# Five edits at the end of an attention kernel: a move split over two queues, a reordered reciprocal and addition, copies by another engine, a last output in halves

## The chip, the cores and the metric

The kernel runs on one core of one Trainium2 chip. The metric is the device time of one execution in microseconds; before the change it is 1126.27 us, the median of three runs (1125.67 to 1128.89). A core has five engines that run their own instruction lists in order and wait for each other by semaphores: TensorE (PE in the profile, its weight loads PEld), VectorE (DVE), ScalarE (ACT), GpSimd (POOL) and SyncE (SP), which here only issues transfers (DMAs). ACT can issue transfers too. Matrix products are summed up in PSUM, other data lie in SBUF.

## What is computed

64 batches of 128 tokens of 512 features pass through one attention layer with a residual. There are 16 heads of 64, one key and one value for all heads, a learned null key and value in front, a causal mask and a mask of tokens. The output is normalized before it is added to the input:

```python
xn = layernorm(x, g_in)
q = (xn @ Wq).reshape(b, n, H, DH).transpose(0, 2, 1, 3) * scale
k, v = split(xn @ Wkv)                      # null key and value put in front
sim = einsum('bhid,bjd->bhij', q, k) + bias # causal and token masks
attn = softmax(sim, axis=-1)
out = einsum('bhij,bjd->bhid', attn, v).transpose(0, 2, 1, 3).reshape(b, n, INNER)
return x + layernorm(out @ Wo, g_out)
```

All arithmetic is float32.

## The kernel before, in words

The order of all instructions is written out by hand. `step(n)` runs for n from -6 to 62, and each step holds work for several batches at different stages: the projections of later batches, the softmax of batch `eb`, the scores of batch `nb`, the values of batch n, and the output of batches before. In the last steps eb = n + 2 and nb = n + 3. With B = 64, B3 = 58. Behind step 62 a few lines finish batches 62 and 63. The lists of the engines keep the order in which `step` calls its helpers.

For one batch b the stages are these:

- `scores` (L495) multiplies queries and keys on PE into `ps`, one buffer, in two halves of the queries; `scores_add` (L508, DVE) adds them to the tile `s`, which POOL has filled with bias and masks; `scores_max` (L513, DVE) takes the maxima. A later half's scores can only start when the addition has read `ps`.
- `exps` (L522, ACT) takes the exponentials, one instruction for each of 8 rows in each half, and sums them. `rinv` (L539, DVE) is the reciprocal of the sums and `scale` (L543, POOL) multiplies by it.
- `blocks_T` (L575, DVE) transposes blocks of 32x32 from `s` into `sb`, and `blocks_move` (L601) moves them in 14 transfers into `aTb`. There are two tiles `aTb` for the last batches, used in turn. With `take=0` only the even-numbered seven of the transfers are issued, by SP; with `take=1` the odd-numbered seven, by ACT. Before the change only batch 63 is split in this way.
- `values` and `values_end` (L636, PE) multiply `aTb` with the values into two tiles `po`, and two copies with a bias (L680, ACT) bring them to `oT`.
- The output product with `wo`: up to batch 58 two batches at a time, by a scheme with seven products of half size (`out_sums` on POOL, `out_product` L750 on PE, `out_part` L773 on DVE, or L771 on ACT). Then follow `pair_stats`, the power -0.5 on POOL (`pair_pow`), `pair_nmr` (L794, DVE), `pair_norm` (L804, ACT into `yn`) and `pair_residual` (L808 and L809, DVE). From batch 59 on it is `out_mm` (L697, PE: 8 products of 512 columns into `py`), `out_stats` (L813 to L820, DVE), `residual` (L834 on ACT, L835 on POOL), `store` (L838, SP).

The residual's input is loaded a second time into `res`, of which there are two buffers (L126, SP): the load for a batch must wait until the batch two before it in these loads has been added. SP's list in steps 59 and 60 is: moves of 60, res(58), res(59), moves of 61, stores of 57 and 58, res(60), moves of 62, SP's half of the moves of 63. ACT's list from step 58: yn(55), first half of the exponentials of 60, oT(58), yn(56), second half of 60, all of 61 (with one copy between), oT(59), exponentials of 62 with the copy that completes y(58) and yn(57) between, yn(58), oT(60), the residual of 59, exponentials of 63, oT(61), seven moves of 63, the residual of 60, oT(62).

Of the kernel before, what the change touches and what calls it, by code (L numbers as in the profile page):

```python
# [17 lines left out]
def kernel(  # L18
# [654 lines left out]
    def values_end(b, split):  # L673
        g = b // GB
        if split:
            value_mm(b, 1, 1, lo, vs[g], slice(4, 6), start=False)
            value_mm(b, 0, 1, hi, vs[g], slice(2, 4), start=False)
        po = pos.pop(b)
        for u in range(2):
            nc.scalar.activation(  # L680
                oT[b][:, u * NF : (u + 1) * NF, :].rearrange(
                    "p f (s q) -> p s f q", q=Q
                ),
                po[u].rearrange("p h i f q -> p (h i) f q"),
                AF.Identity,
                bias=nv2,
            )

    def out_mm(b, lo=0, hi=NC):
        if lo == 0:  # L690
# [44 lines left out]
    def out_product(p, k, pool, tag, start=True):  # L735
        key = "y" + tag
        if start:
            prod[key] = pool.tile([P, HE], FP, tag=tag, name=f"py{tag}_{p}_{k}")
        a, b = oT[p], oT[p + 1] if p + 1 in oT else None
        h, w = {  # L740
            1: lambda: (a[:, lo_c], e11),
            2: lambda: (a[:, hi_c], e21),
            3: lambda: (a[:, hi_c], e22),
            4: lambda: (b[:, hi_c], wT[:, 3]),
            5: lambda: (yS[p], wT[:, 0]),
            6: lambda: (a[:, lo_c], wT[:, 1]),
            7: lambda: (b[:, lo_c], wT[:, 2]),
        }[k]()
        for c in range(HC):
            nc.tensor.matmul(  # L750
                prod[key],
                h[:, c, :],
                w[:, c, :],
                start=(start and c == 0),
                stop=(c == HC - 1),
                skip_group_check=not start,
            )
# [39 lines left out]
    def pair_norm(b):  # L797
        if b not in nmrs:
            pair_nmr(b)
        nmr, rstd = nmrs.pop(b)  # L800


        yn[b] = ps_y.tile([P, DIM], FP, tag="Y", name=f"yn_{b}")
        nc.scalar.activation(yn[b], ys[b], AF.Identity, bias=nmr, scale=rstd)  # L804
# [6 lines left out]
    def out_stats(b):  # L811
        st = small.tile([P, 6], FP, tag="st", name=f"sto_{b}")
        nc.vector.bn_stats(st, ys[b])  # L813
        mv = small.tile([P, 2], FP, tag="mvo", name=f"mvo_{b}")
        nc.vector.bn_aggr(mv, st)
        rstd = small.tile([P, 1], FP, tag="rstdo", name=f"rstdo_{b}")
        nc.vector.tensor_scalar(rstd, mv[:, 1:2], EPS, None, ALU.add)
        nc.gpsimd.tensor_tensor(rstd, rstd, nhalf, ALU.pow)
        y = hp.tile([P, DIM], FP, tag="y", name=f"y_{b}", bufs=3)
        nc.vector.scalar_tensor_tensor(  # L820
            y, ys.pop(b), mv[:, 0:1], gob, ALU.subtract, ALU.mult
        )
        if b == B - 1:

            nc.vector.scalar_tensor_tensor(y, y, rstd, res.pop(b), ALU.mult, ALU.add)
        else:
            yr[b] = y, rstd
        ys[b] = y

    yr = {}  # L830
# [1 line left out]
    def residual(b):  # L832
        y, rstd = yr.pop(b)
        nc.scalar.activation(y, y, AF.Copy, scale=rstd)  # L834
        nc.gpsimd.tensor_tensor(y, y, res.pop(b), ALU.add)  # L835

    def store(b):
        nc.sync.dma_start(out=out[b], in_=ys.pop(b))  # L838
# [40 lines left out]
    def step(n):  # L879
# [131 lines left out]
        if n == B3:  # L1011
            out_keep("X", "yp1", "p1")
            scores(eb, 0)
            scores_add(eb, 0)
            scores_max(eb, 0)
            out_product(p12, 2, ps_w, "w")
            pair_norm(p4)
            pair_residual(p4)
            store(p4)
            out_part(p12, 0, "w", "yp1")  # L1020
            scores(eb, 1)
            scores_add(eb, 1)
            exps_half(eb, 0)
            scores_max(eb, 1)
        elif first:
            out_keep("X", "yp1", "p1")
            out_product(p12, 2, ps_w, "w")
            out_part(p12, 0, "w", "yp1")
# [7 lines left out]
            q_out(qg, f, lo_t, "w", "p1")  # L1036
        if soft and not second:
            exps(eb, 1, 6)
            rinv(eb, 1)
            scale(eb, 1)  # L1040
        if third and n != B3:
            pair_norm(p4 + 1)
        if second:
# [2 lines left out]
        if n == B3 + 1:  # L1046
            rinv(eb, 0)
            scale(eb, 0)
            blocks_T(n + 1)
            blocks_move(n + 1)  # L1050
        if soft and second:
            exps(eb, 1, 4)
            rinv(eb, 1)
            scale(eb, 1)
        for m in mns:
# [28 lines left out]
            pair_nmr(p4 + 1)  # L1084
        if ok(n):
            values(n, split)
        if third and n != B3:
            pair_residual(p4 + 1)
            store(p4 + 1)
        if soft:  # L1090
            blocks_T(eb)
        if sc and n != B3:
            scores_max(nb, 0)
# [2 lines left out]
            keep("a", "u2")  # L1096
        if ok(n) and not split:
            values_end(n, split)
            if n > B3 + 1:
                out_mm(n - 1, NF)  # L1100
        if n == B3:
# [140 lines left out]
    out_stats(B - 2)  # L1242
    residual(B - 2)
    store(B - 2)
    out_mm(B - 1)
    out_stats(B - 1)
    store(B - 1)
# [1 line left out]
_INS = [  # L1249
    "x",  # L1250
# [34 lines left out]
```

## Time and profile before

| | |
|---|---|
| median of three runs | 1126.27 us |
| profiled execution, own time | 1131.23 us |
| its span, first to last instruction | 1129.4 us |
| mean granted TensorE clock | 0.995 |
| busy: PE, DVE, ACT, POOL | 96%, 72%, 60%, 66% |
| matmuls busy, 1040 to 1060 us | 18.15 of 20.00 us |
| 1060 to 1080 | 17.89 of 20.00 |
| 1080 to 1100 | 18.37 of 20.00, clock 0.91 |
| 1100 to 1130 | 22.44 of 30.00, clock 0.98 |

A row of the timeline gives the start in us from the start of the span, how long the group of instructions took, the engine, the line of the code, the operation, what it writes and reads, the shape and the count; in brackets how long the engine had been idle before it and which instruction released it. SPq and ACTq are the issues of transfers by SP and ACT. A row of the waits gives who waited for whom, the total in us, how often, and the longest. A row of stretches gives the stretch, its length, the busy time of PE, PEld, DVE, ACT and POOL (with counts), the granted clock (1.00 is full), the share of the transfer engines and GB/s.

### The profile page before, as it was taken

What the parts mean: (1) busy time and instruction counts of PE and PEld (TensorE: products, weight loads), DVE (VectorE), ACT (ScalarE), POOL (GpSimd) and SP (SyncE); (2) the same over time, 40 slices, a digit from 0 to 9 for tenths busy, and PEclk for the clock granted to TensorE, in tenths of its full rate; (3) what the DMA queues carried; (4) which work ended last, traced back from release to release, by engine and by line L of the source; (5) the groups of instructions that cost most, each with busy time, mean ns of one, the idle gap of its engine ahead of it and who ended that gap; (6) DMA issues with size and microseconds to landing.
All of it is one profiled execution on the core that took longest, in us unless ns stands there. A gap on an engine that the chain in (4) does not pass through costs nothing.

```text
span 1129.4 us, 27505 instructions
## 1 busy us (share of the span) xinstructions
PE 1089.5 (96%) x9780; PEld 873.0 (77%) x9780; DVE 808.0 (72%) x1741; ACT 678.1 (60%) x2710; POOL 745.3 (66%) x588
## 2 busy tenths in 40 slices
PE   6988999999999999999999999999999999999987
PEld 4565788888888888788888888888888888888643
DVE  6564677777787777678777768877777886666852
ACT  2345656666765666676565667566566756657651
POOL 5454877767675776767577676757768575777832
PEclk9999999999999999999999999999999999999999
DMA  6313244363454436345343533534353353422333
GB/s 186 121 33 96 63 128 115 93 168 98 128 131 127 118 91 169 98 124 133 122 123 91 165 105 120 132 120 118 100 163 104 125 134 99 114 75 76 96 104 101
DMA packets 107864, 130.09 MB, mean 115 GB/s; under 512 B 29264, under 2 KB 72528, under 8 KB 105936
## 3 DMA queue, kind: packets, MB, share of 16 engines
q1 hardware_dynamic: 106480, 126.96, 40.0%
q8 instruction: 78, 1.28, 0.5%
q10 hardware_dynamic: 1248, 1.38, 0.4%
q14 instruction: 58, 0.48, 0.1%
HBM read 54.86 MB, written 31.46 MB: 76 GB/s over the span
## 4 chain that ended last, share of the span: by engine, by line
PE 68%; DMA 8%; POOL 7%; DVE 6%; SPq 5%; issue 3%; ACT 3%; POOLq 0%; ACTq 0%; DVEq 0%
PE pa L422 14%; PE pyX L750 13%; PE pc L422 7%; PE ps L495 7%; PE po L636 6%; PE pyY L750 6%; DMA x<-in_x_dram 6%; PE pk L308 4%; SPq L601 4%; PE pw L422 3%; PE pyw L750 3%; PE py L697 3%; ACT s L522 2%; POOL s L543 1%; POOL xS L404 1%
## 5 line engine op out<-in xcount | busy, mean ns | idle before, releaser
L522 ACT ACTIVATE s<-s,nmax 128x65 f32<-128x65 f32 (+1 forms) x1024 | 372.2, 368 | 0.4
L466 POOL TENSOR_TENSOR s<-biasp,mneg 128x1536 f32<-128x1536 f32 x64 | 221.1, 3455 | 110.0 <-DVE sb L575 99.0
L543 POOL TENSOR_TENSOR s<-s,rinv 128x512 f32<-128x512 f32 (+1 forms) x128 | 189.2, 1479 | 119.5 <-DVE nmro L794 86.8
L680 ACT ACTIVATE oT<-po,nv 128x512 f32<-128x512 f32 x128 | 81.0, 683 | 203.2 <-PE po L636 203.2
L522 ACT ACTIVATION_READ_ACCUMULATOR s<-s,nmax 128x1 f32 x1024 | 195.2, 191 | 0.0
L750 PE MATMUL pyX<-wT,oT 128*128 128x256 f32 x696 | 164.7, 379 | 0.5 <-DVE kyu L762 0.5
L750 PEld LDWEIGHTS pyX<-wT,oT 128*128 128x128 f32 x696 | 131.9, 190 | 19.4 <-DVE kyu L762 0.9
L508 DVE TENSOR_TENSOR s<-ps,s 128x512 f32<-128x512 f32 (+1 forms) x128 | 121.6, 950 | 14.2 <-PE ps L495 13.3
L495 PEld LDWEIGHTS ps<-kT,qT 64*64 64x64 f32 x4096 | 92.2, 134 | 46.8 <-DVE s L508 24.9
L422 PE MATMUL pa<-xS,wq 128*128 128x256 f32 x480 | 123.7, 380 | 2.0 <-POOL wq L390 1.0
L513 DVE TENSOR_REDUCE nmax<-s 128x8 f32<-128x520 f32 (+1 forms) x128 | 120.2, 939 | 5.1 <-POOL s L475 3.7
L495 PE MATMUL ps<-kT,qT 64*64 64x64 f32 (+1 forms) x4096 | 116.6, 251 | 3.3 <-DVE s L508 2.6
L575 DVE STREAM_TRANSPOSE sb<-s 128x1536 f32<-128x1536 f32 x62 | 110.0, 1774 | 11.6 <-POOL s L543 4.6
L636 PE MATMUL po<-aTb,vs 64*64 64x256 f32 (+1 forms) x1240 | 114.2, 380 | 2.2 <-DVE done L668 2.2
L433 ACT COPY ku<-pa 128x256 f32<-128x256 f32 x120 | 44.7, 372 | 94.4 <-PE pa L422 94.4
L422 PEld LDWEIGHTS pa<-xS,wq 128*128 128x128 f32 x480 | 86.7, 190 | 12.2 <-ACT ku L433 1.6
L308 PE MATMUL pk<-wkv,xT 128*128 128x144 f32 x488 | 70.2, 287 | 0.0
L422 PE MATMUL pc<-xS,wS 128*128 128x256 f32 x240 | 63.2, 386 | 6.9 <-POOL xS L404 6.9
L422 PE MATMUL pa<-xS,wS 128*128 128x256 f32 x240 | 68.8, 409 | 0.0
L443 DVE TENSOR_TENSOR qT<-pw,kp 128x256 f32<-128x256 f32 x60 | 25.4, 424 | 59.8 <-ACT kp L433 59.7
L636 PEld LDWEIGHTS po<-aTb,vs 64*64 64x64 f32 (+1 forms) x1240 | 55.9, 134 | 12.2 <-issue 3.8
L246 POOL TENSOR_TENSOR rstd<-rstd,nhalf 128x1 f32<-128x1 f32 x64 | 35.8, 559 | 44.5 <-DVE rstd L245 44.4
(120 smaller groups left out, 2105.9 us busy)
## 6 DMA issues: line engine op xcount, KB each, us to landing
aTb<-sb SPq DMA_DIRECT2D x369, 64.0 KB
x<-in_x_dram SPq DMA_DIRECT2D x64, 256.0 KB
res<-in_x_dram SPq DMA_DIRECT2D x64, 256.0 KB
out_dram<-y SPq DMA_DIRECT2D x64, 256.0 KB
aTb<-sb SPq DMA_DIRECT2D x492, 32.0 KB
xd<-xb SPq DMA_DIRECT2D x14, 1024.0 KB
xT<-xd SPq DMA_DIRECT2D x56, 256.0 KB
wo<-in_L_cond_Wo_dram SPq DMA_DIRECT2D x1, 2048.0 KB
```

The lines of the kernel that those rows point to most:

```text
L308: nc.tensor.matmul(pkv, xT[g][:, t, kc, :], wkv[:, kc, :], start=(kc == 0), stop=(kc == KC - 1),)
L422: nc.tensor.matmul(prod[tag], w[:, kc, f * P : (f + 1) * P], t[:, :, kc, :], start=(start and kc == 0), stop=(kc == HK - 1), skip_group_ch ...
L466: nc.gpsimd.tensor_tensor(S[b][:, :, 1 : ROW - 1], biasp, mneg[g][:, t].unsqueeze(1).broadcast_to([P, R8, NL + N]), ALU.add,)
L495: nc.tensor.matmul(pv[u * DH : (u + 1) * DH, r, f, :], qT[g][rows, f, t, hf, u], kT[b][rows, 0:nk], start=True, stop=True,)
L508: nc.vector.tensor_tensor(sv, pss.pop((b, hf)), sv, ALU.add)
L513: nc.vector.tensor_reduce(nmax[b][:, hf], S[b][:, :, WITH_NULL[hf]], AX.X, ALU.max, negate=True)
L522: nc.scalar.activation(row, row, AF.Exp, bias=nmax[b][:, hf, k : k + 1], accum_out=rsum[b][:, hf, k : k + 1],)
L543: nc.gpsimd.tensor_tensor(sv, sv, rinvs.pop((b, hf)).unsqueeze(2).broadcast_to([P, R8, sv.shape[2]]), ALU.mult,)
L575: nc.vector.transpose(sb.rearrange("p j e q -> p e j q"), S[b][:, :, 1 : ROW - 1].rearrange("p e (j k) -> p e j k", k=Q),)
L636: nc.tensor.matmul(pos[b][u][r * DH : (r + 1) * DH, half], vals[keys, b % GB, 0:DH], aT_of(b)[keys, slots, r * NF : (r + 1) * NF], start=s ...
L680: nc.scalar.activation(oT[b][:, u * NF : (u + 1) * NF, :].rearrange("p f (s q) -> p s f q", q=Q), po[u].rearrange("p h i f q -> p (h i) f q"),
L750: nc.tensor.matmul(prod[key], h[:, c, :], w[:, c, :], start=(start and c == 0), stop=(c == HC - 1), skip_group_check=not start,)
```

## The change

Five edits, all at the end of the program.

1. In step 58 `out_part(57, 0)`, the first half of the features of y(57), comes ahead of the norm, residual and store of batch 55.
2. In step 59 the moves of batch 60 are split: seven are issued by SP at the old place, and seven by ACT behind the exponentials of batch 61. Before, SP issued all 14.
3. In step 60 the reciprocal and the scaling of the second half of batch 62 come behind the addition of the scores of batch 63 and the values of 60. In step 61 those of batch 63, and its transposes, come behind the values and the copies of batch 61.
4. The two copies of `values_end` are made by DVE for batches 61 and 62.
5. The output of batch 63 is computed in two halves of 256 features, each with 8 products into a PSUM tile of its own. Statistics are taken of each half and aggregated, the subtraction, the multiplication and the addition run for each half, and each half has its own store.

```diff
@@ values_end
         for u in range(2):
-            nc.scalar.activation(
-                oT[b][:, u * NF : (u + 1) * NF, :].rearrange(
-                    "p f (s q) -> p s f q", q=Q
-                ),
-                po[u].rearrange("p h i f q -> p (h i) f q"),
-                AF.Identity,
-                bias=nv2,
-            )
+            o = oT[b][:, u * NF : (u + 1) * NF, :].rearrange("p f (s q) -> p s f q", q=Q)
+            v = po[u].rearrange("p h i f q -> p (h i) f q")
+            if b in (B - 3, B - 2):
+                nc.vector.tensor_scalar(o, v, nv2, None, ALU.add)
+            else:
+                nc.scalar.activation(o, v, AF.Identity, bias=nv2)
@@ out_stats
-        if b == B - 1:
-            nc.vector.scalar_tensor_tensor(y, y, rstd, res.pop(b), ALU.mult, ALU.add)
-        else:
-            yr[b] = y, rstd
+        yr[b] = y, rstd
@@
+    def last_output():
+        b = B - 1
+        halves = []
+        st = small.tile([P, 2, 6], FP, tag="st2", name="st2", bufs=1)
+        for e, (pool, tag) in enumerate(((ps_y, "Y"), (ps_w, "w"))):
+            cols = (lo_e, hi_e)[e]
+            py = pool.tile([P, HE], FP, tag=tag, name=f"py_{b}_{e}")
+            for c in range(NC):
+                nc.tensor.matmul(
+                    py,
+                    oT[b][:, c, :],
+                    wo[:, c, cols],
+                    start=(c == 0),
+                    stop=(c == NC - 1),
+                )
+            nc.vector.bn_stats(st[:, e], py)
+            halves.append((py, cols))
+        mv = small.tile([P, 2], FP, tag="mvo", name=f"mvo_{b}")
+        nc.vector.bn_aggr(mv, st)
+        rstd = small.tile([P, 1], FP, tag="rstdo", name=f"rstdo_{b}")
+        nc.vector.tensor_scalar(rstd, mv[:, 1:2], EPS, None, ALU.add)
+        nc.gpsimd.tensor_tensor(rstd, rstd, nhalf, ALU.pow)
+        y = hp.tile([P, DIM], FP, tag="y", name=f"y_{b}", bufs=3)
+        for py, cols in halves:
+            nc.vector.scalar_tensor_tensor(
+                y[:, cols], py, mv[:, 0:1], gob[:, cols], ALU.subtract, ALU.mult
+            )
+        r = res.pop(b)
+        for py, cols in halves:
+            nc.vector.scalar_tensor_tensor(
+                y[:, cols], y[:, cols], rstd, r[:, cols], ALU.mult, ALU.add
+            )
+            nc.sync.dma_start(out=out[b][:, cols], in_=y[:, cols])
@@ step
             out_product(p12, 2, ps_w, "w")
+            out_part(p12, 0, "w", "yp1")
             pair_norm(p4)
             pair_residual(p4)
             store(p4)
-            out_part(p12, 0, "w", "yp1")
             scores(eb, 1)
@@
         if soft and not second:
             exps(eb, 1, 6)
-            rinv(eb, 1)
-            scale(eb, 1)
+            if n <= B3 + 1:
+                rinv(eb, 1)
+                scale(eb, 1)
@@
             blocks_T(n + 1)
-            blocks_move(n + 1)
+            blocks_move(n + 1, take=0)
         if soft and second:
             exps(eb, 1, 4)
+            if n == B3 + 1:
+                blocks_move(n + 1, take=1)
             rinv(eb, 1)
             scale(eb, 1)
@@
             values(n, split)
+        if n == B3 + 2:
+            rinv(eb, 1)
+            scale(eb, 1)
         if third and n != B3:
             pair_residual(p4 + 1)
             store(p4 + 1)
-        if soft:
+        if soft and n != B3 + 3:
             blocks_T(eb)
@@
             values_end(n, split)
+            if n == B3 + 3:
+                rinv(eb, 1)
+                scale(eb, 1)
+                blocks_T(eb)
             if n > B3 + 1:
                 out_mm(n - 1, NF)
@@ end of the program
-    out_mm(B - 1)
-    out_stats(B - 1)
-    store(B - 1)
+    last_output()
```

## The prediction

> **What bounds the kernel now.** I read the end of the program only, since every edit lies behind 1050 us. Times are us from the start of the span (1129.4), and I name work by its batch. First the timeline: TensorE (PE) has work without a break up to 1054 us, and from there these are its larger gaps, with the instruction that ended each:
>
> ```profile
> 1055.39 0.65 PE L636 MATMUL po<-aTb,nv 64*64 64x256 f32 x4 [0.89 <-DVE y L773]
> 1056.67 1.26 ACT L680 ACTIVATE oT<-po,nv 128x512 f32<-128x512 f32 x2 [0.42 <-PE po L636]
> ...
> 1078.58 0.43 PE L636 MATMUL po<-aTb,nv 64*64 64x256 f32 x2 [0.92 <-DMA aTb<-sb]
> ...
> 1081.32 1.98 PE L495 MATMUL ps<-kT,qT 64*64 64x128 f32 x32 [1.66 <-DVE s L508]
> ...
> 1097.06 3.70 PE L697 MATMUL py<-wo,oT 128*128 128x512 f32 x8 [0.31 <-ACT oT L680]
> ...
> 1102.14 0.65 PE L636 MATMUL po<-aTb,nv 64*64 64x256 f32 x4 [0.80 <-DMA aTb<-sb]
> ...
> 1108.04 3.70 PE L697 MATMUL py<-wo,oT 128*128 128x512 f32 x8 [0.61 <-ACT oT L680]
> ```
>
> In order: the values of 58 wait for VectorE (DVE), those of 60 for their moves, the scores of 63 for an addition, the output of 61 for oT, the values of 62 for their moves, the output of 62 for oT. The reader should see how small they are: 5.2 us in all. Behind 1108 nothing waits until the tail.
>
> Next the sync queue (SP), because the chain of waits runs through it from 1093 to 1102 us, issue by issue:
>
> ```profile
> 1067.15 9.89 SPq L601 DMA_DIRECT2D aTb<-sb  x14
> 1077.09 2.74 SPq L126 DMA_DIRECT2D res<-in_x_dram  x2
> 1079.92 9.91 SPq L601 DMA_DIRECT2D aTb<-sb  x14
> 1089.88 1.09 SPq L838 DMA_DIRECT2D out_dram<-y  x2
> 1091.01 0.46 SPq L126 DMA_DIRECT2D res<-in_x_dram  x1
> 1091.58 15.74 SPq L601 DMA_DIRECT2D aTb<-sb  x21
> ```
>
> These are the moves of 60, the loads res(58) and res(59), the moves of 61, two stores, res(60), then the moves of 62 and half of those of 63. From 1079.9 on SP issues without rest, and the last move of 62 lands at 1102.05, which ends the 0.80 wait. So **the start of the moves of 61 sets the end**. What sets that start is in the list of SP's waits:
>
> ```profile
> SPq L126 <- DVE y L809: 1.7, 1, 1.7
> ```
>
> res(59) needs the buffer of res(57), free when DVE has added y(57), 1078.77 to 1079.46. Then come 22 us of SP work. Anything that delays y(57) arrives at the end; SP being done sooner with 60 doesn't help while it waits there.
>
> Last, stretches of 3.41 us laid on the clock's own steps (PE busy, ..., granted clock):
>
> ```profile
> 1057.41:1060.82 3.41, 2.12 (x55) 1.62 (x46) 3.06 (x7) 3.40 (x13) 2.95 (x4) 1.00 0.24 59
> ...
> 1077.89:1081.30 3.41, 1.08 (x12) 0.57 (x12) 2.31 (x6) 3.00 (x14) 1.48 (x3) 1.00 0.51 133
> 1081.30:1084.71 3.41, 3.39 (x41) 2.51 (x42) 3.13 (x5) 0.73 (x2) 1.27 (x1) 0.50 0.36 97
> ```
>
> After a stretch with 1.08 us of matmuls the next one ran at half clock, which costs half of 3.41, 1.7 us; after one with 2.12 it did not.
>
> **The change part by part.**
>
> *1. Half of y(57) ahead of the norm of 55 (step 58).* DVE now has to take L773 before nmro(55). L773 reads pyw, whose matmuls end at 1051.05 + 1.99 = 1053.04. So L773 (0.41) runs 1053.08 to 1053.49, nmro ends at 1053.62, and ScalarE (ACT) starts yn(55) at 1053.65 instead of 1052.77: 0.88 late. The eight exponentials of 60 behind it end at about 57.1, so oT(58) starts there and not at 1056.67, although its values, freed from the 0.89 wait, are ready about 0.5 sooner than before. On DVE the reciprocal of (60, first half) waits for those exponentials, 57.2 instead of 56.38, and pushes the maxima and nmro(56) from 57.64 to 58.46. ACT takes yn(56) at 58.69, not 57.94: **0.75 late**. From there ACT has no gap up to the last exponential of 61 at 1067.78, so 0.75 stays, and with it the transposes of 60 and 61. Ends: -0.4 (if only the 0.42 wait of oT goes) and +0.88. I take +0.75, because each link is an in-order queue with its own row.
>
> *2. Moves of 60 from two queues (step 59).* Seven of 14 leave SP; SP is done at about 1072.5 instead of 1077.0 and then waits at res(59) as before. ACT issues the other seven behind the exponentials of 61 (1067.87 + 0.75 = 68.6) and ahead of oT(59). The nearest row is the move of 63, which already goes this way:
>
> ```profile
> 1100.56 6.03 ACTq L601 DMA_DIRECT2D aTb<-sb  x7
> ```
>
> Seven issues held ACT for 6.03 us, the shortest 0.60, the median 0.74, one of 1.43. ACT was free from 1067.9 to 1071.39 (3.52 of wait for the values of 59), so that much is hidden and no more. With seven at 0.74 (5.2) ACT is free at 73.85. Queued behind: oT(59) (1.26), four exponentials of 62 (1.35), the copy that completes y(58), six more exponentials; then yn(57). So oT(59) 73.9 to 75.15, y(58) at 76.85, the exponentials to 78.9, yn(57) at 78.93 instead of 1077.22: 1.71 late, 0.96 of it from this edit. At 0.60 plus gaps (4.5 us) it would be 0.2, at 6.03 it is 1.85. I take the median, **+0.96**.
>
> The Trainium skill speaks against this edit. "DMA: Bandwidth & Descriptors", section "Issuing engines are not separate DMA queues", says that issuing from several engines saves only the time of issuing. By the rows, two queues took 6.7 us for 63 and one took 9.9 for 60; 3.2 sooner would remove the 0.92 wait of the values of 60, and the edit would come to +0.96 - 0.92, nearly nothing. By the rule only SP's issue time is saved, and SP spends that waiting for y(57): +0.96 stays. I take the rule's sum, since the removed wait lies before the SP queue, which is late.
>
> *3. Reciprocal and scaling of (62, second half) behind the addition of 63 (step 60).* DVE waited 0.92 for ACT there, with the addition behind. Now the addition follows y(57) at once: about 81.2 to 81.9, against 81.27 at its end before. Without this edit it would be 1.7 late, with it 0.65. PE has run the values of 60 in one piece to about 80.4, so its stretch stays above 2.1 busy of 3.41 and the half clock should not follow. PE reaches the values of 61 at about 90.7 instead of 91.44. The moves of 61 land at about 93.6 (1.7 late), so this is hidden: **0**. If SP were not late, it would be worth up to 1.06 plus 1.7 of clock. For 63, one step on, the reciprocal now stands behind oT(61), which is done before the exponentials are; 0.
>
> *4. oT(61) and oT(62) by DVE.* No row shows DVE in this form; a 128x512 addition from PSUM takes 0.69, so two take 1.4 against 1.25 on ACT. DVE is idle there (2.9 and 5.3 us of waits). oT(62) no longer stands behind ACT's seven issues: **-0.61**. The 0.31 before 1097 goes too, but in front of the values of 62, whose moves are late: 0. Ends -0.5 to -0.95.
>
> *5. Last output in halves.* Matmuls stay alike: 16 of 256 columns at 0.43 against 8 at 0.86. The tail before:
>
> ```profile
> 1123.88 0.70 DVE L813 BATCH_NORM_STATS2 sto<-py 128x6 f32<-128x512 f32 x1 [5.10 <-PE py L697]
> ...
> 1125.75 0.75 DVE L825 SCALAR_TENSOR_TENSOR y<-y,rstdo,res 128x512 f32<-128x512 f32 x1
> ```
>
> Half the statistics lie under the matmuls: 0.70 becomes about 0.40 (a 256-wide addition takes 0.42 against 0.69). The four half passes cost about 0.15 more than two whole ones, so DVE ends near 0.2 sooner. The second store starts behind the first's issue (0.33), so little sooner than the old one, but it carries 128 KB, and the last 256 KB took 0.8 us on the engines: 0.4 less. Together **-0.5** (0 to -0.8).
>
> Sum: +0.75 + 0.96 - 0.61 - 0.5 = +0.6. The profiled execution took 1131.23 us, 1.8 more than its span; it becomes 1131.8. It stands 5 us above the median of the runs, 1126.27; the difference carries over: **1126.9 us**.
>
> **The rivals.**
>
> *A, y(57) not late.* Edit 1 costs nothing and ACT issues at 0.60. Then SP keeps its times and only 4 and 5 count: -1.1, 1125.2. For it: ACT's 3.52 of rest. Against it: 7 x 0.60 is over that already.
>
> *B, the gaps close.* PE sets the end: 0.92 + about 1 of the 1.66 + 1.7 of clock + 0.31 + 0.61 + 0.5 are about 5 at most; I take -3.9, 1122.4. It needs the SP chain to start 3 us sooner, and no edit moves y(57) forward; I find nothing for that but a wrong reading of edit 1.
>
> *C, half clock (slower).* The lateness turns into two PE waits, before the values of 61 (moves land near 93.6) and of 62 (near 103.75), of 1.2 to 2 us. If one lies in one stretch of 3.41 so that too little is busy, the next runs at half clock: +1.7 each, 1128.6 for one and 1130.3 for two. By the rows it decides somewhere between 1.08 and 2.12 busy; a wait of 2 leaves 1.4. Here the skill's rule ("TensorE: Matmul & The Clock Gate", section "HAM oscillation") is that gaps above some 3.4 us matter; by it C never happens, +0. The row has it happen with gaps of 0.92 and 1.66, so I keep C.
>
> *D, the queues don't run side by side*, ACT's moves waiting for SP's to land: the upper end of edit 2, +1.5 in all, 1127.8; counted with the forecast.
>
> **How the numbers follow.** Forecast with D 0.45, A 0.24, B 0.15, C 0.16. The likeliest one's own range is 1125.0 to 1127.9 (edit 1 at -0.4 and 2 at 0.2; both at their top). For 8 in 10 I reach to 1123.2, leaving most of B out, and to 1129.5, leaving C with two stretches out. The bound of 0.3%, about what a measurement of this kernel can tell from no change, is 3.4 us: below 1122.9 lies B, 0.15 with its neighbours; above 1129.65 most of C with a slow ACT, 0.14; within, 0.71.
>
> **What would show it.** yn(55) near 53.6 and oT(58) near 57.1 (edit 1); seven ACT issues of 5 to 6 us before oT(59), and y(57) 1 to 2.5 us late, with SP idle before res(59) (edit 2); no half clock at 1081 (edit 3); no wait before the output of 62 (edit 4); the waits for moves before the values of 61 and 62 grown past 1 us. I am wrong if y(57) comes at its old time or sooner, or if SP issues faster than 0.6 to 0.7 us a move.

## The result, and the profile after

| | before | after |
|---|---|---|
| median of the runs made side by side (20 each) | 1129.29 us (1125.58 to 1131.84) | 1130.87 us (1127.48 to 1134.37) |
| profiled execution, own time | 1131.23 | 1131.52 |
| its span | 1129.4 | 1129.7 |
| mean granted clock | 0.995 | 0.992 |

The ratio is **1.0021, 95% interval 1.0011 to 1.0031**: the change made the kernel slower, by some 2.4 us by this ratio and by 1.6 us between the two medians, inside the bound of 0.3%. One run of all that follow, of e6_345_res (1867.84 us), was in a slow state and is left out of its ratio. Two things of this table matter for what follows. The kernel before ran 3 us above the three runs that the forecast was tied to (they are among these twenty, and were low draws), and it did so again beside every experiment (1128.96 to 1129.37). And the runs of one kernel lie over 6 us apart, so a single profile is one draw. Much of that spread arises before any edit counts: in the twenty profiles of this study the first scores of batch 60, ahead of which nothing was changed, start anywhere from 1046.63 to 1052.06 us.

The gaps of TensorE (PE) in the profile of after, to be held against those of before:

```profile
1056.43 0.69 PE L495 MATMUL ps<-kT,qT 64*64 64x64 f32 x32 [1.53 <-DVE s L508]
1058.59 1.98 PE L495 MATMUL ps<-kT,qT 64*64 64x128 f32 x32 [1.46 <-DVE s L508]
...
1082.53 1.10 PE L495 MATMUL ps<-kT,qT 64*64 64x128 f32 x32 [2.08 <-DVE s L508]
...
1092.87 0.65 PE L636 MATMUL po<-aTb,nv 64*64 64x256 f32 x4 [1.16 <-DMA aTb<-sb]
...
1103.72 0.65 PE L636 MATMUL po<-aTb,nv 64*64 64x256 f32 x4 [1.54 <-DVE y L819]
```

The last three are about what was forecast: the waits ahead of the outputs of 61 and 62 (0.31 and 0.61) are gone, and those for the moves of 61 and 62 have grown past 1 us. (The last names a VectorE instruction. But the values come 10.70 us behind the start of the moves of 62, and 10.71 to 10.73 behind it in e13_again and e14_look below, in e18_eleven, where another instruction is named, and in e2_no_split, where the moves are; I read it as a wait for the moves.) The first two are new. In before, PE waited 0.89 us for the output of 57 ahead of the values of 58. Edit 1 removed that wait, so the values are done sooner, and PE now stands in front of the next scores, whose buffer VectorE (DVE) has not yet read. What follows is seen in the stretches laid on the clock's steps (here the eighth figure, after the busy times of five engines, is the granted clock):

```profile
1054.47:1057.89 3.42, 1.12 (x36) 0.56 (x32) 3.24 (x7) 3.16 (x15) 2.14 (x4) 1.00 0.31 71
1057.89:1061.30 3.41, 2.71 (x35) 2.30 (x36) 3.06 (x6) 3.27 (x14) 3.25 (x3) 0.50 0.27 65
1061.30:1064.71 3.41, 3.41 (x10) 2.69 (x9) 2.19 (x4) 3.41 (x21) 3.01 (x3) 0.50 0.38 109
...
1078.37:1081.78 3.41, 2.08 (x50) 1.13 (x48) 2.46 (x8) 3.14 (x15) 2.10 (x3) 1.00 0.02 5
1102.26:1105.67 3.41, 1.95 (x13) 1.00 (x14) 1.97 (x6) 0.00 (x0) 0.55 (x1) 1.00 0.48 109
```

The two new pauses fell into one stretch and left 1.12 us busy in it, and the clock was halved for 6.83 us, in the stretch in which the output of 57 is made. The stretch at 1078 kept 2.08 us busy, and the half clock that before had at 1081 is gone.

ScalarE (ACT) and SP then show the chain that the forecast described. ACT's seven issues of the moves of 60, and the copy oT(59) behind them:

```profile
1068.58 5.60 ACTq L601 DMA_DIRECT2D aTb<-sb  x7
1074.29 1.27 ACT L686 ACTIVATE oT<-po,nv 128x512 f32<-128x512 f32 x2 [6.33 <-DMA aTb<-sb]
```

SP's queue, and what it waits for at the load of the residual of 59:

```profile
1068.62 4.57 SPq L601 DMA_DIRECT2D aTb<-sb  x7
1073.23 8.88 SPq L126 DMA_DIRECT2D res<-in_x_dram  x2
1082.21 9.06 SPq L601 DMA_DIRECT2D aTb<-sb  x14
...
1093.02 16.89 SPq L601 DMA_DIRECT2D aTb<-sb  x21
```

```profile
SPq L126 <- DVE nmro L793: 8.0, 1, 8.0
```

```profile
1081.06 0.69 DVE L808 TENSOR_TENSOR y<-yn,res 128x512 f32<-128x512 f32 x1
```

SP issues its half of 60 in 4.57 us, where all of it took 9.89, and then stands for 8 us (1.7 before) until y(57) is added, at 1081.75 by the last row; the name in the wait is the DVE instruction beside that. The moves of 61 start 0.46 us behind it. In the tail, the last statistics are now over half the columns, 0.43 us where before they took 0.70:

```profile
1124.63 0.43 DVE L848 BATCH_NORM_STATS2 st<-py 128x6 f32<-128x256 f32 x1 [3.02 <-PE py L841]
...
1126.21 0.87 DVE L862 SCALAR_TENSOR_TENSOR y<-y,rstdo,res 128x256 f32<-128x256 f32 x2
```

**Where the time went.** To compare profiles I count from the start of the first scores of 60 (1050.42 us in before, 1049.70 in after), which no edit reaches. Two further profiles of the change, e13_again and e14_look, stand beside it:

| us after the first scores of 60 | before | after | e13_again | e14_look |
|---|---|---|---|---|
| ACT's issues of 60 start; how long | none | 18.88; 5.60 | 17.49; 6.44 | 18.34; 5.60 |
| oT(59) starts | 20.97 | 24.59 | 24.04 | 24.04 |
| y(57) done | 29.04 | 32.05 | 31.12 | 31.51 |
| moves of 61 start | 29.50 | 32.52 | 31.58 | 31.97 |
| moves of 62 start | 41.16 | 43.32 | 42.38 | 42.76 |
| values of 62, second part | 51.71 | 54.02 | 53.10 | 53.47 |
| PE ends | 73.42 | 74.90 | 75.62 | 76.04 |
| span ends | 79.02 | 80.03 | 80.76 | 81.18 |
| half clock begins, up to PE's end (3.41 us each) | 30.9 | 8.2, 11.6 | 54.5 | 10.7, 55.1 |

Reading the columns as differences gives the account of each profile:

| step, us against before | after | e13_again | e14_look |
|---|---|---|---|
| start of the moves of 61 | +3.02 | +2.08 | +2.47 |
| from there to the moves of 62 (before had 11.66, the others here 10.8) | -0.86 | -0.86 | -0.87 |
| from there to the values of 62 | +0.15 | +0.17 | +0.16 |
| from there to PE's end | -0.83 | +0.81 | +0.86 |
| tail | -0.47 | -0.46 | -0.46 |
| sum | +1.01 | +1.74 | +2.16 |

The sums are of the size that the runs give, +2.4 us here (interval 1.2 to 3.5) and +1.2 in the repetition below. The +0.8 in the fourth row is -0.83 with one stretch of half clock on top. The second row can't be put down to the edits: e3_345, e4_only_split and e5_only_part below, with fewer of them, have 10.76 to 10.79 there, and e2_no_split has 11.31.

### The profile page after: what moved, and what is told of

It is laid out like the page before. It is cut to its first block, busy times and chain, and to the rows that moved or that the text cites. A ratio compares the mean times of both kernels' runs of the same rounds, so it can differ in the third digit from the quotient of the medians.

```text
span 1129.7 us, 27545 instructions
## 1 busy us (share of the span) xinstructions
PE 1090.7 (97%) x9796; PEld 878.1 (78%) x9796; DVE 812.1 (72%) x1748; ACT 675.5 (60%) x2706; POOL 745.5 (66%) x588
## 3 DMA queue, kind: packets, MB, share of 16 engines
q10 hardware_dynamic: 1680, 1.71, 0.5%
## 5 line engine op out<-in xcount | busy, mean ns | idle before, releaser
L686 ACT ACTIVATE oT<-po,nv 128x512 f32<-128x512 f32 x124 | 78.5, 684 | 203.1 <-PE po L636 196.7
L575 DVE STREAM_TRANSPOSE sb<-s 128x1536 f32<-128x1536 f32 x62 | 109.9, 1773 | 10.8 <-POOL s L543 3.7
```

Source lines behind the costliest of these rows:

```text
L575: nc.vector.transpose(sb.rearrange("p j e q -> p e j q"), S[b][:, :, 1 : ROW - 1].rearrange("p e (j k) -> p e j k", k=Q),)
L686: nc.scalar.activation(o, v, AF.Identity, bias=nv2)
```

## The experiments

All were timed in five rounds beside the kernel before, except two single runs. In the diffs, a minus is a line of the kernel named.

### The parts of the change

The change without edit 1 (e1_no_part), without edit 2 (e2_no_split), and without both, which leaves edits 3 to 5 (e3_345):

```diff
 # without edit 1
-            out_part(p12, 0, "w", "yp1")
             pair_norm(p4)
             pair_residual(p4)
             store(p4)
+            out_part(p12, 0, "w", "yp1")
 # without edit 2
-            blocks_move(n + 1, take=0)
+            blocks_move(n + 1)
...
-            if n == B3 + 1:
-                blocks_move(n + 1, take=1)
```

> The change without edit 1: the half of y(57) stands behind the norm of 55 again. Theory P (edit 1 carries most of the loss: it makes ScalarE and VectorE about 0.8 us late and opens a pause of PE at step 58 that can halve the clock): the loss of 2.4 us against before falls to about +0.3 or below, no half clock between 1054 and 1065 us in the profile, and y(57) is at most 1 us later than before. Theory S (edit 2 carries it: ScalarE is held by seven issues, and y(57) and the moves of 61 come late): the loss stays at +1.5 to +2.4, with y(57) 1 us or more late. Theory T (edits 3 to 5 carry it): stays at +2.

> The change without edit 2: all 14 moves of 60 are issued by SP. Theory S: the loss falls to about 0 to +0.5, oT(59) follows the values of 59 at once. Theory P: the loss stays at +1 to +2, oT(58) again 0.45 us later than in before against its surroundings and yn(56) 0.8 later. Theory T: stays at +2.

> Edits 3, 4 and 5 alone. Theories P and S both: 1.1 us faster than before (the wait of 0.61 ahead of the output of 62 gone, the tail 0.5 shorter), or a little more through the addition of 63 that no longer waits for the reciprocal. Theory T: slower than before by 1 to 2 us.

The kernel before with the split of edit 2 alone (e4_only_split) and with edit 1 alone (e5_only_part), by the same lines put in:

> Before with edit 2 alone. Theory S (ScalarE is held by seven issues, y(57) and with it the moves of 61 and 62 come late): 0.5 to 1.5 us slower than before; in the profile oT(59) starts 2 to 3 us late, the moves of 61 1 to 2 us late, and the second half of the values of 62 comes 10.6 us after the moves of 62 start, as in all profiles so far. Rival: the two queues bring the moves of 60 sooner, and the kernel is up to 1 us faster.

> Before with edit 1 alone. Theory P: 0.8 to 2 us slower than before; yn(56) 0.8 us late, PE with pauses of about 1.5 and 1.5 us at step 58 in place of 0.89 and 0.82, and in about half of the executions a stretch at half clock behind them. Rival: PE gains the 0.89 us and the kernel is up to 0.5 us faster.

| | ratio to before | oT(59) | y(57) done | half clock begins |
|---|---|---|---|---|
| e1_no_part | 1.0010 [0.9995, 1.0024] | 22.56 | 29.64 | 51.9 |
| e2_no_split | 1.0013 [1.0004, 1.0021] | 21.75 | 29.83 | 30.7 |
| e3_345 | 1.0003 [0.9990, 1.0016] | 20.95 | 29.03 | 52.6 |
| e4_only_split | 1.0015 [1.0004, 1.0027] | 22.57 | 29.66 | 31.9 |
| e5_only_part | 1.0014 [1.0003, 1.0026] | 24.00 | 32.08 | 8.2, 11.6 |

Each of edits 1 and 2 alone makes the kernel before slower, by an amount whose interval lies above 1. Where the clock held, edit 1 moved y(57) by 0.80 us (e2_no_split against e3_345: 29.83 and 29.03) and edit 2 by 0.61 (e1_no_part: 29.64). The forecasts of these runs put nearly the whole loss on one edit, and neither came: without edit 1 the kernel is +1.1 us against before, without edit 2 +1.5. The effects do not simply add. In e5_only_part there is no split at all, but the half clock at step 58 is there, and y(57) is done at 32.08, the time of the full change (32.05): oT(59) needs both ACT free of its issues and the values of 59 done, and the later of the two counts. Taking away one of them therefore gains little.

Two rows ask for more. e3_345 was expected 1.1 us below before, by edits 4 and 5, and took +0.3 (interval -1.1 to +1.8): their gain is not seen in the mean. In its profile y(57) is at its old time, and PE still waits 1.17 us ahead of the values of 61 and 1.54 ahead of those of 62, as in after; half clock followed, and from the values of 62 to PE's end it took 22.54 us, where after took 20.88. And e4_only_split is +1.7 us although its y(57) is only 0.62 late. In its profile the output of 62 waits 1.69 us for oT(62) (0.61 in before), which stands behind ACT's seven issues of 63. Edit 4 takes that wait away, but its worth depends on these issues: in e5_only_part, without edit 4, they took 4.88 us instead of before's 6.03, PE did not wait there, and from the values of 62 to PE's end it took 20.89 us.

Edits 4 and 5 alone (e10_only_45), that is e3_345 without edit 3:

```diff
-            if n <= B3 + 1:
-                rinv(eb, 1)
-                scale(eb, 1)
+            rinv(eb, 1)
+            scale(eb, 1)
...
-        if n == B3 + 2:
-            rinv(eb, 1)
-            scale(eb, 1)
...
-        if soft and n != B3 + 3:
+        if soft:
             blocks_T(eb)
...
-            if n == B3 + 3:
-                rinv(eb, 1)
-                scale(eb, 1)
-                blocks_T(eb)
```

> The order of the kernel before with edits 4 and 5 alone (results of 61 and 62 copied by VectorE, the last output in two halves). Theory: the way from the values of 62 to the end of TensorE is 20.9 us as in the change (21.7 before), and the tail behind it 5.1 instead of 5.55, so 1.3 us or 0.11% are gained where the clock is the same; with a half clock behind the values of 62 some 0.7 to 1.7 of it is given back. Edit 3 at nothing: as edits 3 to 5 together (1.0003) within 0.1%. Rival (edit 3 is what brings the half clock at the values of 62 in the runs without the split): no half clock there, and 0.1% faster than before.

It took 1133.05 us, 1.0035 [1.0023, 1.0047], the slowest of all, and neither view was right. DVE's rows show why:

```profile
1096.15 0.20 DVE L539 RECIPROCAL rinv<-rsum 128x8 f32<-128x8 f32 x1 [2.88 <-ACT s L522]
1098.43 1.78 DVE L575 STREAM_TRANSPOSE sb<-s 128x1536 f32<-128x1536 f32 x1 [2.08 <-POOL s L543]
1100.13 1.37 DVE L684 TENSOR_SCALAR oT<-po,nv 128x512 f32<-128x512 f32 x2
```

The copy of 61 stands in DVE's queue behind the reciprocal and the transposition of 63, which wait for ACT and for POOL. On ACT it had stood behind the exponentials alone. PE meanwhile stood before the output of 61:

```profile
1100.90 2.08 PE L696 MATMUL py<-wo,oT 128*128 128x512 f32 x2 [4.47 <-DVE oT L684]
```

Behind this pause the clock was halved for 6.83 us, from 1098.90. So the second half of edit 3, which puts the reciprocal and the transposition of 63 behind the copy of 61, is what edit 4 needs. This run leaves out the first half too; that the second carries the loss is read from these rows, and no run has edit 3 alone.

### The queue of SP

The load of the residual of 59 is put behind the moves of 61, so that these no longer wait for y(57). Four kernels have this edit: e6_345_res (on edits 3 to 5), e9_after_res (on the change), e8_only_res (on the kernel before) and e11_res_split (on the change without edit 1).

```diff
-        if 0 <= n and plain(n):
+        if 0 <= n and plain(n) and n != B3 + 1:
             load_res(n)
...
         if eb in sbs:
             blocks_move(eb)
+        if n == B3 + 1:
+            load_res(n)
```

> Edits 3, 4 and 5, and the load of res(59) issued behind the moves of 61 instead of ahead of them, so that those moves no longer wait for y(57). If the start of the moves of 61 sets the end (the chain through SP), the moves of 61 start near 1077.7 instead of 1079.9, those of 62 land about 2 us sooner, the wait of 0.80 ahead of the values of 62 goes, and the kernel is 2 to 3 us faster than before. If PE sets the end anyway, it is as fast as edits 3 to 5 alone.

> The change with the load of res(59) issued behind the moves of 61. If y(57) sets the end through the SP queue, the moves of 61 start near 75 instead of 82 us, the waits ahead of the values of 61 and 62 go, and the kernel is 2 to 3 us faster than the change, near or below before. If not, it is as slow as the change.

> The kernel before with one difference: the load of the residual of 59 is issued behind the moves of 61. Theory (the moves of 61 set the end): they start 2 to 2.2 us earlier than the 29.5 us of before, as with edits 3 to 5 beside it (27.3), and the time falls by 0.05 to 0.2%. Rival (the gain of that run came from edits 3 to 5, which by themselves gave 1.0003): no change within 0.05%.

> The changed kernel without its edit 1 (the half of the output of 57 is back behind the residual of 55) and with the load of the residual of 59 behind the moves of 61. Theory (edit 1 costs by the pauses of TensorE at step 58, the split of the moves costs only through the output of 57 and so through the moves of 61 behind the residual's load): the clock at step 58 stays full, the moves of 61 start at about 25 us after the first scores of 60 (with the residual of 59 ahead of them 30.1), and the time is 0.2 to 0.45% below the kernel before and 0 to 0.2% below the changed kernel with the late residual (0.9979 of before). Rival (edit 1 is harmless in itself once nothing waits for the output of 57): the same as that kernel within 0.1%. Second rival (without edit 1 the late stretch of half clock comes back at the values of 62): 0 to 0.1% above it.

| | ratio to before | moves of 61 start | values of 62 | PE ends |
|---|---|---|---|---|
| e6_345_res | 0.9991 [0.9981, 1.0001] | 27.32 | 49.84 | 70.71 |
| e9_after_res | 0.9979 [0.9970, 0.9989] | 24.66 | 50.03 | 71.93 |
| e8_only_res | 0.9999 [0.9989, 1.0008] | 26.68 | 50.33 | 72.35 |
| e11_res_split | 0.9967 [0.9955, 0.9979] | 22.77 | 48.88 | 70.33 |

SP's queue in e9_after_res:

```profile
1067.87 4.56 SPq L601 DMA_DIRECT2D aTb<-sb  x7
1072.47 0.61 SPq L126 DMA_DIRECT2D res<-in_x_dram  x1
1073.62 10.40 SPq L601 DMA_DIRECT2D aTb<-sb  x14
```

Between its half of the moves of 60 and the moves of 61 it now has only the load of the residual of 58. y(57) is as late as ever there (32.04), and the half clock at step 58 is the same, yet the kernel is 0.42% below the change. The same move of the load took only 0.12% off edits 3 to 5 (e6_345_res, 1.0003 to 0.9991), so the larger part of the 0.42% goes with the late y(57): in the change, its way to the end did lead through SP's queue, as the forecast had it. With this order the split of edit 2 pays, since SP's sooner end is used: e11_res_split is e6_345_res with the split, and takes 0.9967 where that takes 0.9991. It is the best version found: 1125.11 us, **0.33% below the kernel before** (0.21 to 0.45); against e9_after_res, which has edit 1 too, the intervals overlap. In its profile the moves are in time, and PE has only these pauses over half a microsecond behind 1064 us:

```profile
1073.25 3.70 PE L696 MATMUL py<-wo,oT 128*128 128x512 f32 x8 [1.80 <-ACT oT L686]
1080.37 1.10 PE L495 MATMUL ps<-kT,qT 64*64 64x128 f32 x32 [1.88 <-DVE done L668]
```

On the kernel before (e8_only_res) the late load gave nothing that can be told from zero, as the rival had said. Its moves of 61 start 2.8 us sooner and PE ends 1.1 us sooner in its profile. Other waits are still there: 2.33 us ahead of the scores of 63 with half clock behind it (from 31.2), and 0.32 and 0.93 for the copies of 61 and 62 by ACT. So that the start of the moves of 61 sets the end is shown for the change, and not for the kernel before.

### The clock at step 58

Multiplications of a constant are put into the first new pause of the change: ten (e7_after_fill), then five (e12_fill5, e16_fill_again and the single run e15_fill_look). What they compute is not used. e13_again and e14_look are the change itself once more.

```diff
         if n == B3:
+            pb = ps_q.tile([P, P], FP, tag="a", name="busy58")
+            for _ in range(5):
+                nc.tensor.matmul(pb, ident, ident, start=True, stop=True)
             out_sums(p12)
```

> The change with ten more 128x128 matmuls of a constant into a free tile, in the pause of PE behind the values of 58; they add work to the computation and nothing uses their result. If the pauses that edit 1 opens there cost by the half clock, the mean granted clock rises by about 0.001 against the change, and it is 0.5 to 1.5 us faster than the change. If the lateness of ScalarE and VectorE is all, it is as slow as the change or up to 0.5 slower.

> The changed kernel with five multiplications of a constant behind the sums of 58's values' predecessor at step 58, about 1.25 us of TensorE, which fit into the pause of 1.53 us ahead of the values of 58 (ten took 2.50 us and delayed the scores of 61). Theory (the two pauses of 1.53 and 1.46 us leave 1.1 of 3.4 us busy and halve the clock for 6.8 us, which costs about 2.2 us): no half clock at step 58, the output of 57 ends 30.5 to 31.2 us after the first scores of 60 instead of 32.05, and the time is 0.1 to 0.2% below the changed kernel (1.0021 of before), so 1.000 to 1.001. Rival (the clock at step 58 differs between executions, and is not what the change costs on average): as the changed kernel within 0.05%.

> The changed kernel, unchanged, beside the one with five multiplications in the pause at step 58, on one chip. Theory (the pauses at step 58 halve the clock in most executions, and that costs 1 to 2 us in the mean): its profile shows half clock within 12 us behind the first scores of 60, and its runs lie 0.08 to 0.2% above those of the kernel with the five multiplications. Rival (that half clock is rare, or other stretches come in its place): the two agree within 0.05%.

> The changed kernel with the five multiplications in the pause at step 58 (about 1.25 us of TensorE that compute nothing of use), beside the changed kernel. Theory: no half clock at step 58, and 0.08 to 0.2% below the changed kernel. Rival: the same within 0.05%.

> One more profile of the changed kernel, to count how often the half clock comes at step 58. Theory: there again, 3.4 or 6.8 us of it within 12 us behind the first scores of 60, and the output of 57 at about 32 us; where it is missing, the output of 57 is at 29.8 to 30.5. Rival: no half clock there, and the output of 57 late all the same.

> One more profile of the changed kernel with the five multiplications at step 58. Theory: no half clock within 12 us behind the first scores of 60, and the output of 57 ends at 30.0 to 30.7 us. Rival: half clock there as in the changed kernel.

| | ratio to before | half clock within 12 us | y(57) done | ACT's issues of 60, us |
|---|---|---|---|---|
| after | 1.0021 [1.0011, 1.0031] | yes | 32.05 | 5.60 |
| e13_again | 1.0011 [0.9999, 1.0024] | no | 31.12 | 6.44 |
| e14_look | one run | yes | 31.51 | 5.60 |
| e7_after_fill | 1.0018 [1.0008, 1.0027] | no | 31.02 | 5.05 |
| e12_fill5 | 1.0004 [0.9991, 1.0017] | no | 30.33 | 5.65 |
| e16_fill_again | 1.0012 [1.0002, 1.0022] | no | 29.81 | 5.00 |
| e15_fill_look | one run | no | 31.97 | 7.02 |

My first theory was that the half clock at step 58 explained the result. Edit 1 brings it: of the eight profiles without edit 1 none has half clock within 12 us, of the eight with it and without a filling five have. The fillings remove it, in four profiles of four, and e12_fill5 took the time that was forecast (1.0004). But on one chip the change and the filled kernel took the same time (1.0011 and 1.0012), and that theory **fell as a statement on the mean**: a gain of 0.1% from keeping the clock up there is not shown. e7_after_fill is not a fair test, because its ten multiplications took 2.50 us, more than the pause; five fit.

e13_again tells why. In it the values of 58 came late by themselves, and the pauses were spread out:

```profile
1055.48 0.65 PE L636 MATMUL po<-aTb,nv 64*64 64x256 f32 x4 [0.65 <-DMA aTb<-sb]
1057.49 0.69 PE L495 MATMUL ps<-kT,qT 64*64 64x64 f32 x32 [0.34 <-DVE s L508]
1059.64 1.10 PE L495 MATMUL ps<-kT,qT 64*64 64x128 f32 x32 [1.46 <-DVE s L508]
...
1103.86 0.65 PE L636 MATMUL po<-aTb,nv 64*64 64x256 f32 x4 [1.54 <-DVE y L819]
```

No half clock came of these first pauses, but ACT's issues, started at 17.49 us by the count above, held it for longer:

```profile
1068.25 0.74 ACTq L601 DMA_DIRECT2D aTb<-sb  x1
1069.09 5.60 ACTq L601 DMA_DIRECT2D aTb<-sb  x6
```

That is 6.44 us to the end, and y(57) was late all the same. The issues themselves did not take that long. Singly they take 0.55 to 1.13 us (median 0.64), and seven of them 4.5 to 4.9 us in every profile. What makes the difference is waiting between them. The transfers of SP and ACT share eight semaphores that tell of a landing, and ACT issues a transfer only when the one before it on the same semaphore has landed. In e13_again the third issue waited 1.22 us for the load of a residual that SP had issued, in e15_fill_look 1.69 us for a store and a later one 0.61 for a move, in after one 0.45 for a move; in e16_fill_again none waited, and ACT was held 5.00 us. So e15_fill_look, with full clock, has y(57) as late as after.

And the 1.54 us ahead of the values of 62, the same as in after, fell differently on the clock's steps:

```profile
1101.89:1105.30 3.41, 1.87 (x16) 0.71 (x12) 1.96 (x6) 0.00 (x0) 0.55 (x1) 1.00 0.51 119
1105.30:1108.71 3.41, 3.41 (x7) 1.51 (x5) 1.25 (x2) 0.52 (x1) 0.00 (x0) 0.50 0.17 41
```

In after, the same pause left 1.95 us busy and cost nothing further; here 1.87 was left and the next stretch ran at half clock. From the values of 62 to PE's end it took 22.52 us instead of 20.88.

### A dose of the split

The change with three, and with eleven, of the fourteen moves of 60 issued by ACT instead of seven:

```diff
-                    if take is not None and count % 2 != take:
+                    onact = (count % 4 == 3) == True if b == B3 + 2 else count % 2 == 1
+                    if take is not None and onact != (take == 1):
```

This gives three; for eleven, `True` is `False`.

> The changed kernel, with three of the fourteen moves of 60 issued by ScalarE instead of seven, and eleven by SP. Theory (what edit 2 costs is the time that ScalarE's issues hold it, beyond the 3.5 us that it waited for the values of 59): three hold it 2.2 to 3 us, which fits; oT(59) comes 20.9 to 21.8 us after the first scores of 60 (24.0 to 24.6 in the change), the output of 57 ends at 29.8 to 30.7, and the time is 0.0 to 0.15% below the change's 1.0011 to 1.0021. Rival (a split in any proportion costs the same, through contention of the two queues): the output of 57 at 31 or later, as in the change.

> The changed kernel, with eleven of the fourteen moves of 60 issued by ScalarE instead of seven, and three by SP. Theory: eleven hold ScalarE 7.7 to 10 us, so oT(59) comes at 25.3 to 28 and the output of 57 ends at 32.4 to 35 us after the first scores of 60, the moves of 61 0.46 behind it, and the time is 0.1 to 0.4% above the change. Rival (as above): the output of 57 at 31 to 32.1, and the time of the change.

| moves by ACT | ratio to before | ACT held, us | oT(59) | y(57) done | half clock begins |
|---|---|---|---|---|---|
| 3 | 1.0008 [0.9998, 1.0019] | 2.00 | 23.32 | 31.40 | 10.5, 54.9 |
| 7 (e13_again) | 1.0011 [0.9999, 1.0024] | 6.44 | 24.04 | 31.12 | 54.5 |
| 11 | 1.0025 [1.0016, 1.0035] | 8.77 | 26.37 | 33.45 | 26.3, 29.7, 57.0 |

With eleven, y(57) follows ACT as the theory said, and the time rises. With three I expected y(57) at 29.8 to 30.7 and it was done at 31.40, which is what the rival had said, though ACT was free early: it waited 5.07 us for the values of 59, which the half clock at step 58 had held up. This is the other one of the two ways to oT(59), and without a split that counts. The time moved by 0.17% from three to eleven, and the two intervals just overlap (1.0019 and 1.0016).

## Why the prediction was right and wrong

Three steps failed: the base, the size of the lateness of y(57), and a stretch of half clock that the sum put at nothing.

**The base.** The forecast put the profiled execution at 1131.8 us, and said that the difference of 5 us to the median of three runs "carries over"; this took it to 1126.9. That median was 3 us low as a base: beside each of the experiments the kernel before took 1129.0 to 1129.4. With 1129.3 as the base the forecast of +0.6 would have been 1129.9, and 1 us short of 1130.87; the other 3 us of the miss are the base. That the profiled execution took 1131.52, so near 1131.8, is luck: the first scores of 60 came 0.72 us sooner in it than in before, and the part behind them took 1.01 us more. The two further profiled executions took 1133.33 and 1129.60.

**The size of the lateness.** The chain was right for the change: y(57) ended 0.46 us before the moves of 61 in every profile with the residual's load ahead, and e9_after_res showed what it costs by taking the load away. Its size failed, given as 1.71 us ("yn(57) at 78.93 instead of 1077.22"). It was 3.02, 2.08 and 2.47 in three profiles.

- *Edit 1* was put at +0.75 "because each link is an in-order queue with its own row". With the clock up it was +0.80, and yn(55) and oT(58) came at 3.30 and 6.69 where 3.2 and 6.7 were forecast (53.6 and 57.1 in the forecast's count). What I left out was PE: I noted that the values of 58 would be ready sooner and treated that as unused. Work that ends sooner on an engine that then has to wait makes a pause: 1.53 and 1.46 us in place of 0.89 and 0.82, and two of three profiles of the change had half clock behind them.
- *Edit 2* was put at +0.96 with seven issues in 5.2 us and 6.03 as the upper end (for which the same sum gives +1.74, not the +1.85 written there). In the profiles of the change ACT was held 5.60, 6.44 and 5.60 us, in others from 5.0 to 7.02. At the median of 0.74 an issue was put too long; the waits between them for SP's transfers to land were not in the sum. Without edit 1 it cost +0.61, and it is not an addition to edit 1 but the later of two ways.
- *Edit 3* was put at 0. No run has it alone. The half clock at 1081 was absent in all three profiles of the change, as forecast. That edit 4 needs it I had not priced: edits 3 to 5 took 1.0003 of before, and 4 and 5 without it 1.0035.
- *Edit 4* at -0.61 measured -0.83 from the values of 62 to PE's end where no half clock came; 0.61 of it is the wait that is gone, the rest is not told apart, and the copies take 1.4 as estimated. *Edit 5* at -0.5 measured -0.47. In the mean of the runs neither shows.

**The half clock that the sum put at nothing** was rival C, with a chance of 0.16. It came "before the values of 62" in two of the three profiles of the change, and cost 1.64 and 1.69 us beyond the 20.88 of after, where the forecast said 1.7. But rival C had the wrong reason. It said that the lateness turns into two waits, and e3_345, where y(57) is not late, has the same two. Between the values of 61 and those of 62 PE has 9.3 us of work in after, and SP starts the moves of 62 10.8 us behind those of 61; the wait of 1.54 us is about the difference, whenever y(57) is done. In before, a wait for oT(61) and the wait of 0.80 stood in that place.

The forecast had half clock begin somewhere between 1.08 and 2.12 us busy in 3.41. Stretches with full clock between 1045 us and PE's end in the twenty profiles narrow this: with less than 1.5 us busy the next was at half clock in 10 of 10, from 1.5 to 1.92 in 12 of 24, from 1.95 to 2.2 in none of 13. Busy time alone does not decide: of the stretches in which PE's work ended, eight had 1.41 to 1.85 us busy, and none was followed at once by half clock. A wait of 1.51 to 1.57 us stood ahead of the values of 62 in eleven of the twenty profiles, and half clock followed in seven. So this should have been in the likeliest case, not in a rival. The Trainium skill's rule ("TensorE: Matmul & The Clock Gate", section "HAM oscillation") that PE's gaps matter above some 3.4 us would have excluded this; no single gap behind 1054 us in after is longer than 2.08 us, and the rows decide. Rivals A and B did not come: y(57) was late, and the gaps did not close.

**The Trainium skill's other rule**, that issuing from several engines saves only the time of issuing ("DMA: Bandwidth & Descriptors", section "Issuing engines are not separate DMA queues"), was rightly taken: SP's 5.3 us were saved and spent in waiting. They were of use once nothing in the queue waited for y(57): in the best version the split's saved issue time is a gain.

What stays open: how often each stretch of half clock comes. Three profiles of a kernel can't tell, and the runs lie 6 us apart. Whether the mean result of +1.2 to +2.4 us is shared between the two ways to oT(59) and the late half clock in the proportion of these three profiles isn't settled. Nor is the mean of e2_no_split: it lies 1.5 us above before, while the one profile of it, from the first scores of 60 on, is 0.7 us shorter than that of before.

## What to carry to other kernels

Before splitting transfers over two queues, look at what the relieved queue does next: if its next entry waits for a buffer, the saved time goes into that wait. Moving that one entry (here a load that nobody needed yet) can make the split worth having: it took 0.42% off the changed kernel, and nothing off the kernel before. An order change that lets an engine finish sooner without giving it its next work opens a pause there; add up what is busy in the clock's stretch around it, not only the work that was made late. Removing a wait can open the next one in a place where the clock makes it dearer, as edits 3 to 5 did ahead of the values of 62. When a copy is given to another engine, read what stands ahead of it in that engine's queue and what that waits for, and tie a forecast's absolute time to more than three runs when runs lie 6 us apart.

## What I had not expected of the hardware

The place of the clock's steps of 3.41 us against the program differs between executions of one kernel: the same 1.54 us pause left 1.95 us busy in one and 1.87 in another, and only the second was followed by half clock, worth 1.64 us. Seven issues of small transfers held ACT for anything between 5.0 and 7.0 us while SP was issuing too. The issues made up 4.5 to 4.9 us of it. In the longest cases ACT stood 1.2 to 1.8 us between two issues until a load or a store of SP's on the same semaphore had landed: the two queues are tied by the semaphores that they share in this program.
